# Seven edits to a Mamba layer followed by an attention and convolution layer: loads, state copies, plan constants, last image

## The chip, the cores and the metric

The kernel runs on one core of one Trainium2 chip, in fp32 throughout. The metric is device time in microseconds (us), lower is better: the median over the runs of a kernel. One more execution was recorded by the hardware profiler; durations and stages in this document come from that one.

## The reference, cut to what matters

Four images of 512 channels x 32 x 32 go through two residual layers. Before each layer the image is normalised by groups of 16 channels.

```
x = x + mamba(_gn(x), ...)      # layer 0
x = x + pab(_gn(x), ...)        # layer 1

def mamba(f):                    # tokens: L = 1024, C = 512, d_inner = 1024, 16 states
    xn = layernorm(tokens(f)) * ln_w + ln_b
    xm, z = split(xn @ W_in)
    xs = silu(causal_conv4(xm) + conv_b)
    proj = xs @ W_x                              # 32 dt ranks, 16 B rows, 16 C rows
    dt = softplus(proj[:32] @ W_dt + b_dt);  A = -exp(A_log)
    h[t] = exp(dt[t] * A) * h[t-1] + dt[t] * xs[t] * B[t]     # for each channel and state
    y[t] = sum over states of h[t] * C[t]
    return ((y + xs * D) * silu(z)) @ W_out

def pab(x):
    map = softmax over all pairs of (conv1x1(x, w_center)^T conv1x1(x, w_top))
    x = x + map applied to conv3x3(x, w_bottom)
    return conv3x3(x, w_out)
```

## The kernel before, in words

**Two stages.** Layer 0 for all four images comes first, then layer 1 image by image. The normalised images between the two go through DRAM tiles `x1[b][h]`.

**Layer 0.** An image is 1024 tokens long and is scanned in two halves (h = 0 and 1) of T = 512. The 1024 inner channels are cut in 8 blocks of 128 and taken in pairs (e = 0 to 3). So one image is 8 stretches n = 2e + h, and each stretch is 16 units, one per state s; the four images are 32 stretches of 16 units. In a unit (function `unit`), for each of the two channel blocks j:

- ScalarE makes the decay exp(dt * A) (L746), in SBUF (`da`) or, for six of the 16 states, in PSUM (`u`).
- dt * x * B is made in one of two ways. For ten states (`B_ON_ACT`) ScalarE scales transposed rows (`sc`, L758) and TensorE turns them back into a PSUM tile `u` (L784). For the six others GpSimd multiplies by a broadcast row loaded from DRAM (`dbx`, L773).
- VectorE runs the scan along the tokens (L798). In stretches with h = 0 the last column is saved in `carry_sb` as the start of the half h = 1. For three states (`C_ON_DVE`) the scan's result is in the PSUM tile `u` and each scan is followed by its own one-column copy (L803). For the 13 others the result is in SBUF, and one copy of two columns follows when both scans of the unit are done (L820).
- The product with C is made by VectorE for the three states (L814) and by GpSimd for the others (L826). TensorE then adds the product, transposed, into the PSUM accumulators `y0` and `y1` (L833).

At the end of a stretch, `gate` copies y out (L856), turns it back and multiplies by silu(z). Beside the scans of one image run the group norm and layer norm of the next (`norms`), its input projections and convolutions (`conv1`), its x projections (`params`: 16 matmuls, L652), the projections of z (`gates`), the output projection of the last image (`out_proj`), and a transform of the 3x3 weights of layer 1 (`transform`, 32 pieces, each two ScalarE scalings L1084 and L1085, twelve GpSimd operations, three loads and twelve stores).

**What sets the order.** The order within each engine's queue in layer 0 is written by `Plan.issue`. Every step has a priority in units of the scan (`prio`), an assumed duration and a ring of buffers; the planner walks a simulated clock and, on each engine, takes the step of lowest priority value among those that could start soonest. A transform is a `fill` step. Offsets of priorities lie in `PRM`. GpSimd's, ScalarE's and SyncE's DMA queues run in order too. All rings are small: `u` has four PSUM tiles, `h` and `dbx` four SBUF tiles each, `cbc` (the C rows) six.

**The start.** The first image is loaded in four chunks of channels through SyncE's queue, between loads and stores of the transforms. The small weights are loaded on ScalarE's and GpSimd's queues.

**Layer 1.** For each image: 3x3 convolution `w_bottom` (`conv3`, in a Winograd form: six row positions p in three pairs, four column positions q, 96 weight tiles of 1 MB per convolution kind in all), attention (`attend`), scores of the next image, 3x3 convolution `w_out`, and `finish`, which turns the result back (L1470), adds it to `x1` loaded again from DRAM (L1463, L1475) and stores it (L1480). The order here is the program's order as the framework's own scheduler arranges it.

Of the kernel before, what the change touches and what calls it, by code (L numbers as in the profile page):

```python
# [8 lines left out]
F32 = mybir.dt.float32  # L9
AF = mybir.ActivationFunctionType  # L10
# [5 lines left out]
P = 128  # L16
B, C, HH, WW = 4, 512, 32, 32
L = HH * WW
NCC = C // P
# [11 lines left out]
PRM = dict(fi=4.61, m0=27.7, n0=50.77, nl=1.39, q0=50.1, qg=7.76, c0=53.17, cg=7.07, p0=120.48, e0=6.38, eg=3.72, g0=78.98, gg=9.04, o0=14.48, og=4.13, dl=9.01, t0=10, tg=21.42)  # L31
# [24 lines left out]
class Plan:  # L56
# [5 lines left out]
    HOP, LOAD, SLACK, AHEAD = 0.05, 1.3, 0.05, 17.64  # L62
# [107 lines left out]
def mamba_then_pab_kernel(  # L170
# [33 lines left out]
    nc.sync.dma_start(gm_sb, gmat)  # L204
# [8 lines left out]
    nc.gpsimd.dma_start(wt_sb[:, :, 0, :], w_top.rearrange("(c p) n -> p c n", p=P))  # L213
    nc.gpsimd.dma_start(wt_sb[:, :, 1, :], w_center.rearrange("(c p) n -> p c n", p=P))
    pb_sb = cpool.tile([P, 1], F32, tag="pb", name="pb_sb")
    nc.gpsimd.dma_start(pb_sb[0:PAB], b_top)
    nc.gpsimd.dma_start(pb_sb[PAB:P], b_center)
# [46 lines left out]
    with ExitStack() as l0:  # L264
# [16 lines left out]

        mean_w = wp.tile([P, P], F32, tag="mean_w", name="mean_w")
        nc.vector.memset(mean_w, 1.0 / C)

        def small(src, name, cols):
            t = wp.tile([P, cols], F32, tag=name, name=name)
            nc.scalar.dma_start(t, src)
            return t

        lnw_sb = small(ln_w, "lnw_sb", NCC)  # L290
# [5 lines left out]
        a_sb = small(a_log, "a_sb", NDC * NS)  # L296
# [3 lines left out]
        nc.vector.tensor_scalar_mul(a_sb, a_sb, -1.0)  # L300

        wx_sb = wp.tile([P, NDC, RK + 2 * NS], F32, tag="wx", name="wx_sb")
        nc.scalar.dma_start(wx_sb, w_x.rearrange("(d p) n -> p d n", p=P))
# [4 lines left out]
        for k in range(2):  # L308
            nc.gpsimd.memset(wdt_sb[k], 0.0)
            nc.scalar.dma_start(wdt_sb[k][k * NP : k * NP + RK, :], w_dt)  # L310
# [10 lines left out]
        def dram_set(name, shape, n=B):  # L321
# [8 lines left out]
            "xt": 1, "xs": 10, "win": 2, "yt": 1, "dt": 2, "dtx": 2, "dtxt": 2, "cbc": 6,  # L330
# [30 lines left out]
        carry = [buf(None, None, "") for s in range(NS)]  # L361
# [26 lines left out]
        def norms(b, prio, lag=0.0):  # L388

            t = xts[b] = buf("xt", [P, NCC, L], f"xt_{b}")  # L390
            src = x[b].rearrange("(c p) h w -> p c (h w)", p=P)
            for c in range(NCC):
                step(
                    "SP", 0.3, lambda c=c: nc.sync.dma_start(t()[:, c, :], src[:, c, :]),
                    [], [t], prio, kb=512,
                )
# [27 lines left out]
            def mid():  # L424
# [26 lines left out]
                [stat], [pv], prio, "exp",  # L451
# [121 lines left out]
        def project(b, k, w, name, hs, prio, p=None, at=0, holds=()):  # L573
            t = xts[b]
            return group(
                name,
                [
                    (
                        lambda c=c: w()[:, c, :], lambda c=c: t()[:, c, hs],
                        [w, ready[b][c]],  # L580
                    )
                    for c in range(NCC)
                ],
                prio, hs.stop - hs.start, [t, *holds], p, at,
            )
# [37 lines left out]
        def gates(b, d, prio):  # L623

            w = load_win(b, NDC + d, prio)
            sz = buf("sz", [P, L], f"sz_{b}_{d}")
            for h, hs in enumerate(halves):
                p = project(b, NDC + d, w, f"pz_{b}_{d}_{h}", hs, prio)
                step(
                    "ACT", 0.48,  # L630
                    lambda hs=hs, p=p: nc.scalar.copy(sz()[:, hs], p()),  # L631
                    [p], [sz], prio,
                )
            step(
                "ACT", 0.97, lambda: nc.scalar.activation(sz(), sz(), AF.Silu),
                [], [sz], prio, "silu",
            )
            step(
                "SP", 0.3, lambda: nc.sync.dma_start(szd[b][d // 2][:, d % 2, :], sz()),
                [sz], [szds[b][d]], prio, kb=512,  # L640
            )

        def params(b, prio):
# [3 lines left out]
            for h, hs in enumerate(halves):  # L647
                pp = buf("mm" if b else f"y{h}", [P, T], f"pp_{b}_{h}")
                for d in range(NDC):
                    step(  # L650
                        "PE", MM,
                        lambda d=d, hs=hs, pp=pp: nc.tensor.matmul(  # L652
                            pp()[p0 : p0 + NP, :], wx_sb[:, d, :], xs[b, d]()[:, hs],
                            start=(d == 0), stop=(d == NDC - 1),
                        ),
                        [xs[b, k] for k in range(NDC)] if b and d == 0 else [xs[b, d]], [pp],
                        prio if b else prio - 10 + d + 0.5,
                    )
                step(
                    "ACT", 0.48,  # L660
                    lambda hs=hs, pp=pp: nc.scalar.copy(pr()[:, hs], pp()[p0 : p0 + NP, :]),
                    [pp], [pr], prio,
                )
            step(
# [19 lines left out]
        def delta(b, e, h, prio):  # L684
# [29 lines left out]
            for j in range(2):  # L714
                pt = buf("mm", [P, NK, P], f"pdt_{name}_{j}")

                def turn(j=j, pt=pt):
# [6 lines left out]
                    [pt], [dtxt], prio,  # L724
# [3 lines left out]
        def unit(b, e, h, s, y):  # L728
# [49 lines left out]
            for j, u in enumerate(us):  # L778
                part = parts[j]
                if on_act:  # L780
# [11 lines left out]
                    step("PE", 4 * TR, turn, [sc], [u], prio - 1)  # L792
                else:
                    step("ACT", EXP, lambda j=j, u=u: decay(j, u()), [dt], [u], prio - 1, "exp")

                def scan(j=j, u=u):
# [5 lines left out]
                    if h == 0 and on_dve:  # L802
                        nc.vector.tensor_copy(carry_sb[:, j, s : s + 1], ht[:, T - 1 : T])  # L803

                before, behind = ([carry[s]], []) if h else ([], [carry[s]] if on_dve else [])
                step(
                    "DVE", SCAN + (0.15 if behind else 0.0), scan,
# [9 lines left out]
            if h == 0 and not on_dve:  # L817
                step(
                    "DVE", 0.15,
                    lambda: nc.vector.tensor_copy(carry_sb[:, :, s], hc()[:, :, T - 1]),  # L820
                    parts, [carry[s]], prio - 1, holds=[hc],
                )
# [6 lines left out]
            for j in range(2):  # L829
# [9 lines left out]
                step("PE", 4 * TR, add, [parts[j]], [y[j]], prio, holds=[hc])  # L839
# [87 lines left out]
        xv = [x[b].rearrange("(c p) h w -> p c (h w)", p=P) for b in range(B)]  # L927
# [62 lines left out]
        def first_image(prio):  # L990
# [11 lines left out]
            step("POOL", 1.2, make, [], [pieces, *chunks], prio)  # L1002
            for c in range(NCC):
                for h in range(NH):
# [7 lines left out]
                        [x1s[0][h]], [chunks[c]], prio, kb=512,  # L1012
# [53 lines left out]
        def transform(u, src, k, prio):  # L1066
# [20 lines left out]
            step("ACT", 0.83, scales, [], [ends, mids], prio, fill=True)  # L1087
# [45 lines left out]
        norms(0, -200)  # L1133
# [41 lines left out]
    with ExitStack() as l1:  # L1175
# [15 lines left out]

        brow = []
        for name, src in (("b", b_bottom), ("o", b_out)):
            t = wp.tile([1, C], F32, tag=f"brow_{name}", name=f"brow_{name}")
            nc.scalar.dma_start(
                t.rearrange("o (c p) -> o c p", p=P), src.rearrange("p (c o) -> o c p", o=1)
            )
            nc.scalar.activation(t, t, AF.Copy, scale=2.0 / ALPHA[1])
            brow.append(t)
# [118 lines left out]
        def conv3(name, xg, u, bias, first=None):  # L1318
# [47 lines left out]
            for pair in PAIRS:  # L1366
# [14 lines left out]
                for k, p in enumerate(pair):  # L1381
                    m = {}
                    for q in (2, 1, 0, 3):
                        w = fp.tile([P, NCC, C], F32, tag="u", name=f"uw_{name}_{p}_{q}", bufs=3)
# [21 lines left out]
                    ns.append(n)  # L1406

                if pair == (0, 5):
                    nc.gpsimd.tensor_add(y[0], y[0], ns[0])
                    nc.gpsimd.tensor_add(y[3], y[3], ns[1])  # L1410
                    break
# [44 lines left out]

        def finish(b, y):

            dst = out[b].rearrange("(c p) h w -> p c (h w)", p=P)
            for j in range(NCC):  # L1460
                o = fp.tile([P, L], F32, tag="f4", name=f"o_{b}_{j}")
                for h in range(NH):
                    nc.sync.dma_start(  # L1463
                        o[:, h * T : (h + 1) * T], x1[b][h][j * P : (j + 1) * P, :]
                    )
                ov = o.rearrange("p (i r j k) -> p r k i j", r=4, j=TJ, k=2)
                for rr in range(2):
                    pt = ps.tile([P, 4, P], F32, tag="ps", name=f"po_{b}_{j}_{rr}")
                    for k in range(4):
                        nc.tensor.transpose(  # L1470
                            pt[:, k, :], y[2 * rr + k // 2][:, k % 2, j * P : (j + 1) * P], ident
                        )
                    for k in range(2):
                        o2 = ov[:, 2 * rr + k]
                        nc.vector.tensor_add(  # L1475
                            o2, o2, pt[:, 2 * k : 2 * k + 2].rearrange(
                                "p k (i j) -> p k i j", j=TJ
                            ),
                        )
                nc.scalar.dma_start(dst[:, j, :], o)  # L1480
# [3 lines left out]
        for b in range(B):  # L1484
# [6 lines left out]
            if b + 1 < B:  # L1491
                st, rp = scores(b + 1, image[b + 1])
            finish(b, conv3(f"o{b}", xg, uo, brow[1], v))
# [58 lines left out]
```

## Time and profile before

| what | value |
|---|---|
| median of 3 runs | 3147.45 us (3142.55 to 3149.4) |
| profiled execution: its own time | 3152.2 us |
| profiled execution: its span | 3150.4 us |
| start, until the first `dtx` (the last step before the scans) | 151.94 us |
| 32 stretches of scans, until the copy of the last y | 151.94 to 2095.19 us |
| from there to the first matmul of layer 1's first convolution | 2095.19 to 2136.88 us |
| layer 1, until the last matmul | to about 3134 us |
| PE, DVE, ACT, POOL busy over the span | 89%, 74%, 60%, 69% |
| mean granted TensorE clock | 0.968 |

PE is TensorE, DVE VectorE, ACT ScalarE, POOL GpSimd and SP SyncE. A row of groups gives the line, the engine, the operation, output and inputs, the count, then the busy time, the mean ns of one, and the idle time of that engine just before, with what ended it. A row of the stage table gives the stretch and then, for each engine, busy time and number of instructions, the clock, the share of time the DMA engines moved data and the rate. A row of the timeline gives start, duration, engine, line, operation and, in brackets, the idle time before it.

### The profile page before, as it was taken

The page shows a single profiled execution, that of the slowest core. Times are in us where ns is not written, and L with a number is a line of the kernel's source. Part 1 is how long each engine was busy: PE and PEld are TensorE (multiplying, and loading weights), DVE is VectorE, ACT ScalarE, POOL GpSimd, SP SyncE. Part 2 cuts the span into 40 slices and gives each one's busy share as a digit, 9 for nine tenths or more (in the row PEclk, how much of TensorE's full clock was granted, in tenths as well). Part 3 has the DMA queues.
Part 4 walks back from the last instruction along what each step waited for, and adds up shares of the span by engine and source line. Part 5 has one row for each costly group of instructions (what it writes and reads, how often), then busy time and mean ns, then how long its engine had stood idle before and what let it go on. Part 6 is the DMA issues. An engine that isn't in the chain of part 4 may idle for free. (4 is left out here: it accounts for less than half of the span.)

```text
span 3150.4 us, 36613 instructions
## 1 busy us (share of the span) xinstructions
PE 2801.1 (89%) x11832; PEld 1654.8 (53%) x11832; DVE 2324.9 (74%) x2746; ACT 1896.9 (60%) x3322; POOL 2185.6 (69%) x1207
## 2 busy tenths in 40 slices
PE   4988878989888999888999877779999999999998
PEld 2455656666556656565655655544444444444443
DVE  3488899988999988999987987876275366447344
ACT  3499889998799999789998787752030030020000
POOL 8899898999969999978899998853052142224222
PEclk8999899999999999999999989989999999999999
DMA  6666455577645567745567654457268448628817
GB/s 190 192 186 195 144 152 162 156 226 241 212 118 169 163 204 250 231 114 155 165 192 227 204 172 123 121 139 263 93 225 312 183 147 317 257 74 312 321 61 253
DMA packets 401414, 600.03 MB, mean 190 GB/s; under 512 B 47176, under 2 KB 241992, under 8 KB 376648
## 3 DMA queue, kind: packets, MB, share of 16 engines
q1 hardware_dynamic: 392128, 582.13, 58.8%
q10 hardware_dynamic: 8936, 15.31, 1.3%
q8 instruction: 94, 1.54, 0.2%
q14 instruction: 96, 0.79, 0.1%
q0 software_dynamic: 160, 0.26, 0.0%
HBM read 500.60 MB, written 96.99 MB: 190 GB/s over the span
## 5 line engine op out<-in xcount | busy, mean ns | idle before, releaser
L826 POOL TENSOR_TENSOR da<-da,cbc 128x1024 f32<-128x1024 f32 x288 | 679.4, 2364 | 87.2 <-DVE carry_sb L820 47.4
L758 ACT ACTIVATE sc<-dtxt,bt_sb 128x256 f32<-128x256 f32 x1280 | 557.1, 496 | 49.3 <-PE u L784 48.8
L746 ACT ACTIVATE da<-dt,a_sb 128x512 f32<-128x512 f32 x640 | 439.4, 713 | 70.1 <-PE y L833 69.5
L773 POOL TENSOR_TENSOR dbx<-dtx,bbc 128x1024 f32<-128x1024 f32 x192 | 452.1, 2367 | 30.6 <-DMA bbc<-bcd 8.3
L784 PE MATMUL u<-ident,sc 128*128 128x128 f32 x2560 | 380.6, 282 | 52.4 <-DVE da L798 31.7
L833 PE MATMUL y<-ident,da 128*128 128x128 f32 x2560 | 357.3, 283 | 70.7 <-POOL da L826 68.2
L798 DVE TENSOR_TENSOR_SCAN da<-da,carry_sb,u 128x512 f32<-128x512 f32 x288 | 353.3, 1260 | 82.8 <-PE u L784 82.6
L833 PEld LDWEIGHTS y<-ident,da 128*128 128x128 f32 x2560 | 297.6, 145 | 183.4 <-POOL da L826 134.2
L784 PEld LDWEIGHTS u<-ident,sc 128*128 128x128 f32 x2560 | 302.2, 144 | 160.3 <-issue 41.7
L798 DVE TENSOR_TENSOR_SCAN da<-da,u 128x512 f32<-128x512 f32 x288 | 337.1, 1202 | 37.3 <-PE u L784 37.2
L1389 PE MATMUL m_b<-uw_b,v_b 128*128 128x512 f32 x768 | 339.1, 599 | 10.3 <-DMA uw_b<-u_b 9.4
L1389 PE MATMUL m_o<-uw_o,v_o 128*128 128x512 f32 x768 | 333.5, 595 | 4.3 <-DVE v_o L1311 4.1
L826 POOL TENSOR_TENSOR dbx<-dbx,cbc 128x1024 f32<-128x1024 f32 x128 | 302.8, 2365 | 32.1 <-DVE carry_sb L820 22.6
L381 PE MATMUL pxm<-xt,winc 128*128 128x344 f32 (+2 forms) x768 | 249.6, 469 | 30.5 <-DVE xs L610 13.9
L746 ACT ACTIVATE u<-dt,a_sb 128x512 f32<-128x512 f32 x384 | 252.9, 679 | 34.8 <-DVE da L798 18.9
L833 PE MATMUL y<-ident,dbx 128*128 128x128 f32 x1536 | 217.1, 281 | 43.7 <-POOL dbx L826 31.6
L381 PE MATMUL pz<-xt,winc 128*128 128x512 f32 x512 | 246.2, 599 | 10.5 <-ACT sz L631 3.1
L1389 PEld LDWEIGHTS m_b<-uw_b,v_b 128*128 128x128 f32 x768 | 144.7, 191 | 197.8 <-issue 185.7
L1389 PEld LDWEIGHTS m_o<-uw_o,v_o 128*128 128x128 f32 x768 | 145.5, 190 | 190.5 <-issue 181.2
L833 PEld LDWEIGHTS y<-ident,dbx 128*128 128x128 f32 x1536 | 178.4, 144 | 98.2 <-POOL dbx L826 48.6
L1437 PE MATMUL pat<-y_b,st 128*128 128x512 f32 x512 | 221.7, 593 | 0.1
L1397 ACT ACTIVATE e_b<-m_b 128x512 f32<-128x512 f32 x24 | 14.3, 596 | 320.6 <-PE m_b L1389 299.4
(231 smaller groups left out, 4536.2 us busy)
## 6 DMA issues: line engine op xcount, KB each, us to landing
cbc<-bcd SPq DMA_DIRECT2D x512, 256.0 KB, 3.7
uw_b<-u_b SPq DMA_DIRECT2D x96, 1024.0 KB, 4.9
uw_o<-u_o SPq DMA_DIRECT2D x96, 1024.0 KB, 4.9
bbc<-bcd SPq DMA_DIRECT2D x192, 256.0 KB, 4.1
u_b<-work SPq DMA_DIRECT2D x192, 128.0 KB, 2.3
u_o<-work SPq DMA_DIRECT2D x192, 128.0 KB, 3.1
winc<-in_w_in_dram SPq DMA_DIRECT2D x64, 256.0 KB, 3.8
szd<-sz SPq DMA_DIRECT2D x32, 512.0 KB, 3.6
```

Source lines behind the costliest of these rows:

```text
L381: lambda k=k, lhs=lhs, rhs=rhs: nc.tensor.matmul(p()[:, at : at + cols], lhs(), rhs(), start=(k == 0), stop=(k == n - 1)),
L746: nc.scalar.activation(t, dt()[:, j], AF.Exp, scale=a_sb[:, at : at + 1])
L758: nc.scalar.activation(sc()[:, k], dtxt()[:, k], AF.Copy, scale=bt()[:, at, s : s + 1])
L773: lambda: nc.gpsimd.tensor_mul(hc(), dtx(), b_bc().to_broadcast([P, 2, T])),
L784: nc.tensor.transpose(u()[:, k * P : (k + 1) * P], sc()[:, k, j, :], ident)
L798: nc.vector.tensor_tensor_scan(ht, *((hc()[:, j], u()) if on_act else (u(), hc()[:, j])), carry_sb[:, j, s : s + 1] if h else 0.0, ALU.mul ...
L826: lambda: nc.gpsimd.tensor_mul(hc(), hc(), c_bc().to_broadcast([P, 2, T])),
L833: nc.tensor.matmul(y[j]()[:, k, :], hc()[:, j, k * P : (k + 1) * P], ident, start=(s == 0 and k == 0), stop=(s == NS - 1 and k == NK - 1), ...
L1389: nc.tensor.matmul(m[q], v[:, q, k, c, :], w[:, c, :], start=(c == 0), stop=(c == NCC - 1 and not extra),)
L1397: nc.scalar.activation(e, m[2], AF.Copy, scale=al / 2)
L1437: nc.tensor.matmul(pt, st[m][:, 2 * P * j + h : 2 * P * (j + 1) : 2], xb[m // 2][:, m % 2, :], start=(m == 0), stop=(m == NMC - 1),)
```

## The change

Lines of the changed kernel are shifted by some ten to forty; the text keeps the numbers of the kernel before.

1. **Start.** The four chunks of the first image are the first DMAs on SyncE's queue, before `gmat`. The twelve loads of small weights and of the two score weights move from ScalarE's and GpSimd's queues to SyncE's, behind them. The first norm's steps get spaced priorities (lag 0.01).
2. **Weight scalings behind the first norm.** The ScalarE scalings of all transforms now depend on the first norm's exp (a marker `rooted`), and the projections of z of the first image on the first turned dt x (a marker `begun`).
3. **State copy per scan.** Every scan with h = 0 is followed by its own one-column copy; the two-column copy is gone.
4. **x projections spread.** The 16 matmuls of `params` for images 1 to 3 get priorities 0.29 units apart (`pg`), and start 7.45 units earlier (`p0`).
5. **Turns two units ahead.** The turns into `u` get priority two units ahead of their unit (`kt`) where it was one; the adds into y get 0.64 units more (`ka`).
6. **Other constants.** z projections of the first image earlier and closer (`e0`, `eg`), small shifts of norm, convolution and first image, `cbc` ring of 5.
7. **Layer 1.** The two bias rows are loaded and scaled at the very start (on ScalarE's queue) instead of between the layers. The additions of the last pair into y are cut in halves. The last image loads its `x1` ahead of its last convolution, into buffers of the score tiles; half of its turning back is placed before the last weight's matmuls, the last addition is on VectorE, and the stores alternate between two queues.

```
-PRM = dict(fi=4.61, m0=27.7, n0=50.77, nl=1.39, q0=50.1, qg=7.76, c0=53.17, cg=7.07, p0=120.48, e0=6.38, eg=3.72, ...)
+PRM = dict(pg=0.29, kt=2, ke=1, ka=-0.64, fl=0, fi=-1.28, m0=27.07, n0=50.77, nl=1.81, q0=50.1, qg=7.76, c0=53.17, cg=7.03, p0=113.03, e0=-4.84, eg=3.01, ...)
...
+        first = xtp.tile([P, NCC, L], F32, tag="xt", name="xt_0")
+        for c in range(NCC):
+            nc.sync.dma_start(first[:, c, :], xv[0][:, c, :])
+        nc.sync.dma_start(gm_sb, gmat)
...
-            nc.scalar.dma_start(t, src)
+            nc.sync.dma_start(t, src)
...
-                [stat], [pv], prio, "exp",
+                [stat], [pv] if b else [pv, rooted], prio, "exp",
...
-            step("ACT", 0.83, scales, [], [ends, mids], prio, fill=True)
+            step("ACT", 0.83, scales, [rooted], [ends, mids], prio, fill=True)
...
-                        prio if b else prio - 10 + d + 0.5,
+                        prio + PRM["pg"] * (d + NDC * h) if b else prio - 10 + d + 0.5,
...
-                    step("PE", 4 * TR, turn, [sc], [u], prio - 1)
+                    step("PE", 4 * TR, turn, [sc], [u], prio - PRM["kt"])
...
-                    if h == 0 and on_dve:
+                    if h == 0:
                         nc.vector.tensor_copy(carry_sb[:, j, s : s + 1], ht[:, T - 1 : T])
...
-            if h == 0 and not on_dve:
-                step(
-                    "DVE", 0.15,
-                    lambda: nc.vector.tensor_copy(carry_sb[:, :, s], hc()[:, :, T - 1]),
-                    parts, [carry[s]], prio - 1, holds=[hc],
-                )
...
-                step("PE", 4 * TR, add, [parts[j]], [y[j]], prio, holds=[hc])
+                step("PE", 4 * TR, add, [parts[j]], [y[j]], prio - PRM["ka"], holds=[hc])
...
+                    if pair == (0, 5):
+                        eng = nc.vector if late and k else nc.gpsimd
+                        for c in range(2):
+                            eng.tensor_add(y[3 * k][:, c], y[3 * k][:, c], n[:, c])
...
+        def last(b, xg, v):
+            o = [load_sum(b, j, xp, "st") for j in range(NCC)]
+            def late(y):
+                for j in range(NCC):
+                    turn_back(b, j, o[j], y, 0)
+            y = conv3(f"o{b}", xg, uo, brow[1], v, late)
+            for j in range(NCC):
+                turn_back(b, j, o[j], y, 1)
+                (nc.scalar, nc.sync)[j % 2].dma_start(dst[b][:, j, :], o[j])
```

As the two programs are built, ScalarE's queue has 185 table loads where it had 177. VectorE's has 512 one-column copies where it had 96 of these and 208 of two columns. GpSimd does nine transforms before the first `dtx` where it did ten, and as many as before from the second stretch's `dtx` on. The other counts of computing instructions are the same.

## The prediction, written before the changed kernel was run

> **What bounds the kernel now.** I read the profile in this order: the busy times of the page, the stage table cut at the 32 copies of y (L856), the groups, then the timeline at the three seams (start, between the layers, end). No engine bounds the whole. Layer 1 (2137 to 3134 us) is TensorE at 97%, and the change hardly touches it. In the scans the four engines are nearly level, and the leader changes:
>
> ```profile
> span 3150.4 us, 36613 instructions
> ...
> 152.00:223.26 71.26, 58.71 (x301) 38.71 (x302) 51.93 (x61) 65.59 (x116) 67.64 (x38) 0.93 0.69 189
> ...
> 415.45:477.71 62.26, 48.45 (x287) 34.67 (x286) 60.83 (x80) 53.55 (x93) 58.52 (x29) 1.00 0.57 165
> ...
> 716.19:770.57 54.38, 51.22 (x287) 34.03 (x286) 50.01 (x48) 47.34 (x92) 53.75 (x32) 1.00 0.79 237
> ...
> 899.48:970.87 71.39, 61.98 (x317) 43.80 (x318) 64.08 (x90) 63.04 (x106) 47.13 (x22) 0.95 0.45 132
> ```
>
> Columns: stretch, length, then PE, weight loads, DVE, ACT, POOL. POOL leads n = 0 (67.6 of 71.3) and n = 9 (99%), DVE n = 4 (98%); n = 12 is led by nobody. Over all 32 stretches (1943 us) POOL is busy 1760, DVE 1723, ACT 1690. So an engine's saving counts only in the stretches that it leads.
>
> ```profile
> L826 POOL TENSOR_TENSOR da<-da,cbc 128x1024 f32<-128x1024 f32 x288 | 679.4, 2364 | 87.2 <-DVE carry_sb L820 47.4 <-DVE da L798 20.2 <-PE u L784 4.5
> L798 DVE TENSOR_TENSOR_SCAN da<-da,carry_sb,u 128x512 f32<-128x512 f32 x288 | 353.3, 1260 | 82.8 <-PE u L784 82.6
> L820 DVE COPY carry_sb<-da 128x2 f32<-128x2 f32 x144 | 83.8, 582 | 3.9
> L820 DVE COPY carry_sb<-dbx 128x2 f32<-128x2 f32 x64 | 43.3, 676 | 1.6
> L803 DVE COPY carry_sb<-u 128x1 f32<-128x1 f32 x96 | 15.2, 158 | 3.3
> ```
>
> The two-column copies take 127 us of DVE for almost no data; the one-column ones 0.158 us each.
>
> **The change, part by part** (against the profiled execution, 3152.2 us).
>
> *Start.*
>
> ```profile
> 14.34 0.49 SPq L394 DMA_DIRECT2D xt<-in_x_dram  x1
> 20.35 0.21 DVE L411 BATCH_NORM_AGGREGATE mv_l<-bs_l 128x2 f32<-128x12 f32 x1
> 28.29 0.18 ACT L448 ACTIVATE pv_l<-gdev_l 128x4 f32<-128x4 f32 x1
> 151.94 2.50 POOL L710 TENSOR_TENSOR dtx<-dt,xs 128x512 f32<-128x512 f32 x2 [10.41 <-ACT dt L702]
> 166.22 2.33 DVE L798 TENSOR_TENSOR_SCAN da<-da,u 128x512 f32<-128x512 f32 x2 [20.83 <-PE u L784]
> ```
>
> The last chunk of x is issued at 14.3 because it stands behind stores that wait for POOL. In front, the four chunks are issued by 2.5 (0.4 us each in this timeline); 2 MB at the 320 GB/s that the page's best slices show is 6.5 us, so it lands near 9, statistics end near 10.5 instead of 20.6, and the exp of the first norm (28.5) comes about 14 earlier: 10 from the load, 4 because no scaling and no late weight stands in ACT's queue. Down to the layer norm's end (66.3) the halves no longer interleave: pmu's second half, 4.8 of its 9.6 us, runs under VectorE, and two scalings leave ACT; with the first step's wait I put 7. Sum 21: dt is ready at 130.5. The moved loads: 16 more issues on SP of 0.4 us, 7 us, put the first transform's loads at 13 or so; POOL starts its first transform near 15, as now (13.96). Nine transforms of 12.4 us (spacing in the timeline) end at 130 with two short waits, so `dtx` starts at about 130.5. But one transform fewer is behind us, and POOL leads n = 0: 12.4 of the 21 are paid back there. Left 9. The marker on the z projections lets the first scan follow `dtx` by about 7 us instead of 14.3, but POOL is full either way, so I add only 1: **-10**. Bounds: -5 (eight gates now crowd ACT in n = 0, which is at 92%) and -21.
>
> *State copies.* A rule of the Trainium skill speaks against this part. The row first:
>
> ```profile
> 764.92 4.68 POOL L826 TENSOR_TENSOR da<-da,cbc 128x1024 f32<-128x1024 f32 x2
> 767.43 2.19 DVE L820 COPY carry_sb<-da 128x2 f32<-128x2 f32 x1
> ```
>
> The copy lasts until POOL's operation ends (769.60 and 769.62): it waits for it. "SBUF — State Buffer" (Who interferes with whom) says why: a VectorE copy in the two-port mode and a GpSimd operation exclude each other for a whole instruction. "VectorE: DVE Perf Modes" (What auto-detection actually checks) says when: source and destination in SBUF, with outermost sizes even or equal. L803's 0.158 us are of copies out of PSUM, which the rule exempts; the new ones copy from SBUF, and one column equals one column. By the rule the 416 new copies wait as the 208 do, at 0.61 us mean: 254 us, 127 more than now. By the nearest row in size, L803, they take 416 x 0.158 = 66 us, 61 less. No row shows a one-column copy out of SBUF beside POOL. I take 0.158: a single element has no second half for a second port; both ends stay in the range's reasons. At 61 less, an h = 0 stretch saves its copies' time (2.3 to 10.8 us in the stage table of L820) less 26 x 0.158 = 4.1. In those that DVE leads (n = 2, 4, 6, 12, 20, 30) that sums to 13; in those where POOL or ACT is within 4 us of it (8, 10, 14, 16, 18, 22) to 25, of which I count a third. **-20**, bounds -61 and +85 (two thirds of 127: the h = 0 stretches leave DVE only 98 us of idle time).
>
> *Turns.* DVE waits 119.8 us for turns (L784), 99 without the first. One unit earlier on PE they should meet their scans, but they sit longer in the four `u` tiles, and the adds put off by 0.64 units hold `da` longer, for which ACT already waits 69.5 us. I take a tenth of the 99: **-10**, bounds -50 and +30.
>
> *x projections* (16 x 2 matmuls of 0.43 us in a block of 7 us of PE, three times) spread between turns: **-3**. *Eight more table loads*: the row is 1.28 us with the next ACTIVATE 0.02 after its end (149.51, 1.28; 150.81), 10.3 us of ACT; "ScalarE: Activation LUTs" (What ACT_TABLE_LOAD costs) has 2.66 with the drain, 21. I take the row; ACT leads a third of the stretches: **+3** (by the page +7).
>
> *Between the layers.*
>
> ```profile
> 2099.20 1.24 ACTq L1195 DMA_DIRECT2D brow_b<-in_b_bottom_dram  x1
> 2105.18 0.63 ACT L1198 ACTIVATE brow_b<-brow_b 1x512 f32<-1x512 f32 x1 [8.55 <-DMA brow_b<-in_b_bottom_dram]
> 2107.44 5.71 PE L381 MATMUL po<-xs,wpr 128*128 128x512 f32 x8 [4.60 <-ACT grstd_image L245]
> ```
>
> Without the bias row in ACT's queue the norm's root is 6 us earlier, but VectorE now adds all four output blocks before normalising: twelve more matmul records of 7.4 us from 2102.8, an add, four normalisations of 0.75, 16 matmuls of 6.9 from 2111.8 end at 2118.7, not 2121.75. **-3**.
>
> *End.*
>
> ```profile
> 3134.61 2.36 POOL L1410 TENSOR_TENSOR y_o<-y_o,n_o 128x1024 f32<-128x1024 f32 x1 [11.32 <-DVE n_o L1405]
> 3145.41 1.41 DVE L1475 TENSOR_TENSOR o<-o,po 128x256 f32<-128x256 f32 x4 [5.17 <-DMA o<-x]
> ```
>
> After: 16 early turns of 0.11 put the last convolution result at 3136.3, two adds of 0.67 on DVE, 0.5 of turns, eight adds of 0.41 end at 3141.5 where they end at 3146.8 now. **-5**. The early `x1` loads wait on SyncE for the last score tiles, ahead of weight tile 4 of the last convolution; its buffer is free only at 3054, when these eight issues (3.2 us from 3044) are over: nothing. The halved additions of the other images: nothing, PE has the next image's matmuls there.
>
> Sum: -10 - 20 - 10 - 3 + 3 - 3 - 5 = -48, or 3104 for the profiled execution; the median stands 4.75 below it: **3099**.
>
> **The rivals.** (a) *Only the seams pay* (0.25): POOL, at 91% in the scans, does no less work, so DVE's saving becomes DVE idle time. -10 - 3 - 5, and a few from turns: 3125, range 3112 to 3141. For: POOL's 1760 us and the level loads. Against: POOL itself waits 70 us for L820. (b) *More comes free* (0.18): with short copies POOL's waits for L820 (47.4 + 22.6) and DVE's for turns both shrink by half, and the start keeps 15: 3060, range 3040 to 3079. (c) *Slower: the one-column copies queue behind POOL* (0.08, by the rule above): +85 - 31 gives 3201. It decides at a mean copy of 0.42 us: then 416 x 0.42 - 127 = 48 more on DVE, two thirds of which eats the other 31. (d) *No change* (0.03): a change that does not do what it says; the built order shows the copies, the loads and the turns moved, so only a balance of (a) and some lateness gives it. The likeliest (0.46): 3080 to 3112.
>
> **How the numbers follow.** The measurement can tell 0.2%, 6.3 us, from no change. Faster: 0.46 + 0.18 + 0.25 = 0.89, and a little of (c) when its copies are cheap, 0.90. Same 0.03. Slower 0.07. The range leaves out most of (c) and the far half of (b), and takes in (a) nearly whole: 3061 to 3135.
>
> **What would show it.** In the profile after: last `xt` issue before 3 us; first `dtx` near 130 and the copy of the first y near 213; one-column copies at 0.16 us mean, with none that ends with a POOL operation (above 0.42 the forecast falls to (c)); DVE's wait for L784 below 100; POOL's wait for copies gone but partly turned into waits for scans; last add near 5 us before the place it has now against the last matmul. If the stretches with h = 0 are not shorter by 1 to 3 us each, (a) holds.

## The result, and the profile after

| | before | changed |
|---|---|---|
| median | 3148.43 us (4 runs, 3142.55 to 3156.02) | 3105.28 us (4 runs, 3101.93 to 3106.01) |
| ratio to before | | 0.986, 95% interval 0.9837 to 0.9882 |
| profiled execution: span | 3150.4 us | 3103.9 us |

The change makes the kernel 43 us faster; 3099 was predicted, within 3061 to 3135. The two profiled spans differ by 46.5 us. They are cut here at the same marks as in the prediction:

| part | before | changed | difference | predicted |
|---|---|---|---|---|
| until the first y is copied | 223.26 | 229.17 | +5.9 | -10 |
| stretches n = 1 to 31 | 1871.93 | 1834.78 | -37.2 | -30 (copies -20, turns -10, x projections -3, tables +3) |
| to the first matmul of layer 1's convolution | 41.7 | 39.4 | -2.3 | -3 |
| from there to the last matmuls of the last attention | 906.4 | 898.0 | -8.4 | 0 |
| from there to the end | 107.1 | 102.6 | -4.5 | -5 |

So the sum was right, the two small seams were right, and the first term had the wrong sign. The stage table of the changed kernel, for the stretches that the prediction showed (n = 0, 4, 9 and 12; columns as before: stretch, length, PE, weight loads, VectorE, ScalarE, GpSimd):

```profile
144.10:229.17 85.07, 78.60 (x347) 47.84 (x348) 47.88 (x72) 78.53 (x129) 80.27 (x52) 0.96 0.76 221
...
406.98:467.61 60.63, 51.35 (x290) 38.07 (x289) 57.89 (x91) 54.25 (x93) 58.99 (x30) 0.94 0.55 165
...
699.34:751.31 51.97, 49.68 (x278) 33.68 (x277) 44.69 (x46) 46.32 (x87) 51.50 (x31) 1.00 0.78 251
...
869.56:942.77 73.21, 66.64 (x350) 46.99 (x349) 71.16 (x114) 69.37 (x115) 52.13 (x24) 0.99 0.48 132
```

n = 4, which VectorE led with 98%, is 1.6 us shorter and GpSimd leads it now; n = 9, led by GpSimd, is 2.4 shorter; n = 12 is longer. The largest single gains are elsewhere: n = 2 (77.89 to 64.69), n = 19 (66.83 to 56.40), n = 11 (67.34 to 59.36). Two of them are handed on: n = 20 gives 8.7 back, and n = 11 to 13 together take 199 us in both kernels. Of the 37.2 us, 22.8 are gained in n = 1 to 8.

*The copies.* The groups of the changed kernel:

```profile
L829 DVE COPY carry_sb<-da 128x1 f32<-128x1 f32 x288 | 44.2, 154 | 9.9
L829 DVE COPY carry_sb<-dbx 128x1 f32<-128x1 f32 x128 | 19.7, 154 | 4.4
L829 DVE COPY carry_sb<-u 128x1 f32<-128x1 f32 x96 | 15.2, 158 | 3.3
```

The 416 new copies out of SBUF last 154 ns, at most 157, as long as those out of PSUM: 79 us in all where the copies took 142. The timeline shows two of them beside a busy GpSimd:

```profile
745.88 7.00 POOL L846 TENSOR_TENSOR da<-da,cbc 128x1024 f32<-128x1024 f32 x3
...
746.62 1.20 DVE L824 TENSOR_TENSOR_SCAN da<-da,u 128x512 f32<-128x512 f32 x1
747.85 0.15 DVE L829 COPY carry_sb<-da 128x1 f32<-128x1 f32 x1
...
749.18 0.15 DVE L829 COPY carry_sb<-da 128x1 f32<-128x1 f32 x1
```

GpSimd is busy from 745.88 to 752.88; both copies run and end inside. The rival in which they queue behind GpSimd is out. The rule that spoke for it ("VectorE: DVE Perf Modes" of the Trainium skill, What auto-detection actually checks) puts its condition on outermost sizes other than one, and the prediction left "other than one" out; a copy of one column has no such size beside its partitions, and here the measurement decides: no one-column copy waited.

*The start.* SyncE's queue, ScalarE, VectorE and GpSimd in the timeline of the changed kernel:

```profile
0.72 1.98 SPq L291 DMA_DIRECT2D xt<-in_x_dram  x4
...
3.42 0.47 SPq L299 DMA_DIRECT2D a_sb<-in_a_log_dram  x1
12.26 0.33 SPq L299 DMA_DIRECT2D lnw_sb<-in_ln_w_dram  x1
...
19.47 1.04 SPq L1098 DMA_DIRECT2D work<-in_w_bottom_dram  x2
```

```profile
11.10 0.21 DVE L433 BATCH_NORM_AGGREGATE mv_l<-bs_l 128x2 f32<-128x12 f32 x1
12.27 0.63 ACT L221 ACTIVATE brow_b<-brow_b 1x512 f32<-1x512 f32 x1 [6.26 <-DMA brow_b<-in_b_bottom_dram]
18.33 0.18 ACT L470 ACTIVATE pv_l<-gdev_l 128x4 f32<-128x4 f32 x1
26.05 1.82 POOL L1111 TENSOR_TENSOR work<-work 128x768 f32<-128x768 f32 x1 [21.86 <-ACT work L1103]
138.19 1.06 ACT L728 ACTIVATE dt<-dt 128x1024 f32<-128x1024 f32 x1
144.10 2.49 POOL L736 TENSOR_TENSOR dtx<-dt,xs 128x512 f32<-128x512 f32 x2
157.11 1.22 DVE L824 TENSOR_TENSOR_SCAN da<-da,u 128x512 f32<-128x512 f32 x1 [22.54 <-PE u L810]
```

The statistics end at 11.3 (10.5 predicted). But SyncE issues nothing between 3.9 and 12.26, the moment at which the first bias row has landed. The list of SyncE's waits in this stretch names the cause:

```profile
SPq L299 <- DMA brow_b<-in_b_bottom_dram: 8.4, 1, 8.4
```

The load of `lnw_sb` has no use for the bias row. It is the ninth load of the program, the bias row is the first, and in the trace both count their landing on the same semaphore (the counter by which a program waits): the ninth load is held until the first has landed. The kernel before has the same kind of wait, and its profile showed it; here a load of `winc` waits for `cb_sb`, which came through ScalarE's queue:

```profile
SPq L568 <- DMA cb_sb<-in_conv_b_dram: 1.4, 1, 1.4
```

So in the changed kernel the loads of the first transform are issued at 19.5 (13 was assumed) and GpSimd starts it at 26.05 (15 was assumed). ScalarE's queue is held by the same row: the exp of the first norm ends at 18.51, where 14.5 was predicted. Nine transforms of 12.4 us follow with 6.7 us of gaps, and `dtx`, whose dt is ready at 139.25, waits for GpSimd until 144.10.

### The profile page after: what moved, and what is told of

Its sections match the earlier page's. It is cut to its first block, busy times and chain, and to the rows that moved or that the text cites. A ratio compares the mean times of both kernels' runs of the same rounds, so it can differ in the third digit from the quotient of the medians.

```text
span 3103.9 us, 36778 instructions
## 1 busy us (share of the span) xinstructions
PE 2788.6 (90%) x11832; PEld 1654.8 (53%) x11832; DVE 2273.7 (73%) x2956; ACT 1902.3 (61%) x3331; POOL 2179.9 (70%) x1217
## 5 line engine op out<-in xcount | busy, mean ns | idle before, releaser
L824 DVE TENSOR_TENSOR_SCAN da<-da,u 128x512 f32<-128x512 f32 x288 | 349.2, 1213 | 52.8 <-PE u L810 45.4
L772 ACT ACTIVATE u<-dt,a_sb 128x512 f32<-128x512 f32 x384 | 254.1, 679 | 12.3 <-DVE dbx L824 6.0
L1410 ACT ACTIVATE e_b<-m_b 128x512 f32<-128x512 f32 x24 | 14.3, 596 | 311.9 <-PE m_b L1402 290.6
```

Of the source, the lines that this page charges most:

```text
L772: nc.scalar.activation(t, dt()[:, j], AF.Exp, scale=a_sb[:, at : at + 1])
L824: nc.vector.tensor_tensor_scan(ht, *((hc()[:, j], u()) if on_act else (u(), hc()[:, j])), carry_sb[:, j, s : s + 1] if h else 0.0, ALU.mul ...
```

## The experiments

Each comparison is with the kernel before, run on the same chip; the changed kernel stands at 0.986. A difference between a variant and the changed kernel is one of medians, and is given by ratios or spans too where these say something else. Differences below 0.2% between two variants are not taken for real unless the trace shows the cause.

**State copy per scan alone, on the kernel before.** Two-column copy out, `if h == 0:` and one state marker for each channel block in.

> The kernel before with the state copy per scan alone (512 one-column copies in place of 96 of one column and 208 of two). Theory A (the two-column copies waited for GpSimd, and VectorE's time counts where it leads): VectorE's copies fall from 142 to about 79 us, none of them over 0.2 us, and the kernel gains 15 to 25 us, about 3128. Theory B (GpSimd's work sets the pace of the scans, so VectorE's saved time turns into idle time): the copies are as short, but the gain is below 6 us, 3143 to 3149.

Measured: 3143.28 against 3146.35, ratio 0.9993 (0.9986 to 0.9999). All 512 copies last 153 to 159 ns, yet almost nothing is gained: theory B by its number. But not by its reason. Many stretches with h = 0 are 2 to 4 us shorter (n = 4, 6, 8, 10, 16, 18, 24), and up to the end of n = 8 this kernel is 11.6 us ahead of the kernel before. Then two stretches with h = 1 are longer by 10.9 and 6.5 (n = 9 and 17), and late ones with h = 0 by 4.0 and 7.0 (n = 26 and 30). The stage row of n = 9, then VectorE's waits in it:

```profile
704.56:769.85 65.29, 58.40 (x294) 38.25 (x295) 47.26 (x49) 49.23 (x93) 60.87 (x35) 0.97 0.78 243
```

```profile
DVE res L910 <- PE po L381: 15.9, 4, 5.7
```

A whole block of the output projection has moved from n = 8 into n = 9: 66 records of `po` in n = 9, 29.8 us of TensorE (the kernel before has 47 and 22.9 us there, the changed kernel 48 and 22.3), and none in n = 8 (18 and 17). VectorE, in its fixed order, stands 15.9 us behind four additions to `res` that wait for it. The kernel before has 2.3 us of that in its n = 9, the changed kernel 1.2.

**Two-column copy back, in the changed kernel.**

> The changed kernel with the two-column copy put back; all else stays. Theory A: slower than the changed kernel by 15 to 25 us, about 3125, with copies of up to 2.7 us that end with a GpSimd operation. Theory B: within 6 us of it, 3102 to 3111.

Measured: 3132.06, ratio 0.9954 (0.9941 to 0.9967): 27 us slower than the changed kernel (22.5 by the two spans), as theory A says. Its timeline:

```profile
759.96 4.68 POOL L799 TENSOR_TENSOR dbx<-dtx,bbc 128x1024 f32<-128x1024 f32 x2
...
763.21 1.46 DVE L846 COPY carry_sb<-da 128x2 f32<-128x2 f32 x1
```

The copy ends (764.67) with GpSimd's pair (764.64). The 208 copies take 128.1 us, as before. So the copy is worth 27 us beside the other edits and 3 on the kernel before: something else in the change makes its gain collectable. (Another copy step also changes the written order, so the 27 us are those of waiting and of order together.)

**Turns one unit ahead again, adds not put off.** `kt=2, ka=-0.64` to `kt=1, ka=0`.

> The changed kernel with the turns one unit ahead of their unit again and the adds into y not put off (kt = 1, ka = 0). If the early turns are worth what the prediction gave them: 10 us slower, about 3115, and VectorE's wait for turns rises from some 116 us toward 120 to 140. If they are worth nothing without the freed VectorE, or cost as much by holding tiles as they give: 3103 to 3108. If they carry most of the gain of the scans: 3120 or more.

Measured: 3104.99, ratio 0.9874 (0.9857 to 0.9891). The turns alone are worth nothing that can be told (without them the kernel is 0.3 us faster by the medians, 4 slower by the ratios); VectorE waits for them 115.7 us (101.4 + 14.3) where the changed kernel waits 116.0 (95.8 + 20.2) and the kernel before 121.0 (119.8 + 1.2).

**Bias rows loaded as columns.** The rows leave ScalarE's queue; the columns go behind the small weights and are turned into rows by eight small TensorE matmuls between the layers:

```
-        nc.scalar.dma_start(t.rearrange("o (c p) -> o c p", p=P), src.rearrange("p (c o) -> o c p", o=1))
-        nc.scalar.activation(t, t, AF.Copy, scale=-12.0)
+            nc.sync.dma_start(bcol[:, k, :], src)
...
+                nc.tensor.matmul(pr[:, c * P : (c + 1) * P], bcol[:, k, c : c + 1], ident, start=(c == 0), stop=(c == NCC - 1))
+            nc.vector.tensor_scalar_mul(brow[k], pr, -12.0)
```

> The changed kernel, with the two bias rows of layer 1 loaded as columns (128 pieces of 16 bytes each, on SyncE's queue behind the small weights) and turned into rows by TensorE between the layers, where the changed kernel loads them as rows at the start (512 pieces of 4 bytes each, on ScalarE's queue). Theory A (these 1024 small pieces hold up SyncE's issues from 3.9 to 12.3 us): SyncE issues on without the gap, the first transform starts on GpSimd at about 18 to 19 us in place of 26, the first y is 5 to 8 us earlier, and the total 3098 to 3101. Theory B (SyncE's queue is held up by its own loads of x): the gap stays, the total is within 3 us of 3105.

Measured: 3099.06, ratio 0.9847 (0.9833 to 0.9862). SyncE's queue, ScalarE and GpSimd in its timeline:

```profile
3.62 0.44 SPq L293 DMA_DIRECT2D lnw_sb<-in_ln_w_dram  x1
...
5.65 0.43 SPq L293 DMA_DIRECT2D cb_sb<-in_conv_b_dram  x1
8.09 0.33 SPq L293 DMA_DIRECT2D bdt_sb<-in_b_dt_dram  x1
9.41 0.33 SPq L293 DMA_DIRECT2D dp_sb<-in_d_param_dram  x1
...
14.66 0.18 ACT L466 ACTIVATE pv_l<-gdev_l 128x4 f32<-128x4 f32 x1
21.91 1.80 POOL L1107 TENSOR_TENSOR work<-work 128x768 f32<-128x768 f32 x1 [17.72 <-ACT work L1099]
```

The gap of 8.4 us is gone; 3 us in two pieces remain, and these are waits for the loads of x, so theory B holds for a part:

```profile
SPq L293 <- DMA xt<-in_x_dram: 3.0, 2, 2.0
```

Here too each of the two loads that wait (`bdt_sb`, `dp_sb`) stands eight places behind the chunk of x that it waits for. The exp of the first norm ends at 14.84 (the prediction's number), the first transform starts 4.1 us earlier (less than the 7 to 8 expected), the first y comes at 225.30, 3.9 earlier. The two rows were 1024 pieces of four bytes. "DMA: Bandwidth & Descriptors" of the Trainium skill (Rules for kernel authors) says that a load with a strided last dimension becomes one descriptor, that is one piece, per element. A row landed 11.5 us after its issue here, a column load 1.9. The variant changes piece size, queue and place in the order at once, so what each of them is worth is not shown; what the wait was for is.

**x projections in one block again.** `pg=0.29, p0=113.03` to `pg=0, p0=120.48`.

> The changed kernel with the x projections of images 1 to 3 in one block again (pg = 0, p0 = 120.48). The state copies alone gained 0.1% on the kernel before, and taking them back from the changed kernel lost 27 us, so they need a partner. Theory C (the partner is the spread of the x projections: a block of 7 us of TensorE makes late what freed VectorE could have taken): 15 to 25 us slower than the changed kernel, about 3125, the loss in the stretches where the projections stand. Theory D (the partner is the fit of the written order as a whole, or the small constants): 3103 to 3111, no more than the 3 us that the prediction gave.

Measured: 3107.12, ratio 0.9877 (0.9863 to 0.9891). Theory C is out: the copies do not need the spread as their partner. The difference is 2 us by the medians, 5 by the ratios and none by the spans.

**Four small constants back.** `AHEAD` 17.64 (how far the planner looks ahead), `m0=27.7`, `nl=1.39`, `cg=7.07`.

> The changed kernel with four small constants of the order as they were before (planner's window 17.64, m0 = 27.7, nl = 1.39, cg = 7.07). Theory C: within 5 us of the changed kernel. Theory D (constants were fitted to the copy per scan): 10 to 25 us slower, with single stretches 5 to 12 us longer where a step stands in a queue ahead of its input, as in the kernel before with the copies alone (stretch n = 9, 65.3 us in place of 54.4, VectorE waiting 15.9 us for output projections).

Measured: 3099.83, ratio 0.985 (0.9837 to 0.9864): not slower, if anything faster, so these four constants are no partner that is needed either. They move work between neighbours: n = 12 and 20 become 69.3 and 68.1 (73.2 and 80.3 in the changed kernel), n = 11 and 19 become 67.0 and 67.5 (59.4 and 56.4).

**The old start in the changed kernel.** Loads, queues and order as before; no markers; `e0=6.38, eg=3.72`.

> The changed kernel with the start of the kernel before: chunks of x, small weights and scalings in their old order and queues, no markers, z projections of the first image at their old priorities, bias rows loaded between the layers again. By the prediction's start of -10 and seam of -3 it would be 13 us slower, 3118. By the two traces, which show the first y 5.9 us later after the change, it would be 3 us faster (6 gained at the start, 2.3 lost between the layers, all within the noise of a reordered first image): 3097 to 3106.

Measured: 3110.9, ratio 0.9893 (0.9878 to 0.9908), span 3107.6. The expectation from the two traces was wrong. The first y is indeed earlier, at 222.63, but then:

```profile
284.20:356.23 72.03, 55.47 (x271) 38.05 (x270) 64.40 (x108) 64.06 (x107) 59.24 (x34) 0.86 0.54 164
356.23:417.51 61.28, 52.21 (x298) 41.87 (x297) 55.42 (x65) 57.12 (x103) 56.54 (x33) 0.89 0.51 148
```

n = 2 and 3 take 133.3 us, in the changed kernel 117.5. At the end of n = 3 the changed kernel is 10.5 us ahead (406.98 against 417.51). So the new start pays, later than where it was looked for. Why these two stretches are shorter was not tested. One thing moves with it: ScalarE loads tables twice in n = 2 of the changed kernel and 14 times in n = 0; with the old start it is 8 and 7 times, in the kernel before 7 and 7, at 1.28 us each. (In this variant the loads of the bias rows are issued at the start too, at 6.3 and 9.4 us; the last chunk of x goes out at 16.0, 1.6 us later than in the kernel before.)

**Halved additions alone, on the kernel before.**

> The kernel before with the additions of the last pair into y cut in halves, for all images, on GpSimd; nothing else. The prediction gave them nothing. If TensorE's waits for GpSimd's addition (3.8 us of matmul and 6.3 us of weight loads in layer 1 of the kernel before, three each) are what shortened layer 1 by 8.4 us after the change: 4 to 8 us faster, 3138 to 3142. If the prediction was right: 3144 to 3148.

Measured: 3143.63 against 3146.85, ratio 0.999 (0.9982 to 0.9999): 3 us, below the 4 to 8 expected. TensorE's weight loads wait for that addition, before (without the last image) and then with halves (with it):

```profile
PEld po L1470 <- POOL y_o L1410: 6.3, 3, 2.1
```

```profile
PEld po L1471 <- POOL y_o L1409: 3.9, 4, 1.2
```

Three waits of 2.1 us become three of 0.9, and the last image's, at the very end, goes from 1.5 to 1.2: some 4 us. The rest of the 8.4 cannot be put down to the change. With the copies alone, where layer 1 is untouched, the same part took 899.6 us in its profile where the kernel before took 906.4, with 6.7 us of waiting for weights instead of 9.4; and with the changed layer 1 it took up to 904.8 (the last variant below).

**Copy alone, with the output projection's additions later.** On the first of these variants, `res` and its store get `at + 1.5`.

> The kernel before with the copy per scan, as in the run that gained 0.1%, and with one thing more: VectorE's additions of the output projection (res) and their stores get a priority 1.5 units later. Theory E (in that run the freed VectorE stood at these additions, which wait in its queue for TensorE: 40.8 us in place of 24.2): the wait falls to 25 or less, stretches n = 9 and n = 17 come back to about 54, and the kernel gains 12 to 18 us on the kernel before, 3129 to 3135. Theory F (the loss is TensorE's and GpSimd's work that has moved across the stretch's end): the wait falls, the time stays within 5 us of 3143.

Measured: 3148.39 against 3147.99, ratio 0.9996 (0.9985 to 1.0007). It tested little: in the written order the additions of n = 9 kept their places (only some of the later images moved, by a few scans), VectorE still waits 42.1 us for output projections, and n = 9 takes 66.1. Theory E is neither shown nor refuted by it.

**Turns, x projections and small constants all back, in the changed kernel.** What stays is the start, the copies, layer 1 and the ring of five C rows.

> The changed kernel with turns, x projections and the four small constants all back together; what stays of the change is start, copy per scan, layer 1 and the ring of five C rows. Each alone moved the changed kernel by -5 to +2 us. If the copies need any one of them as a partner: 3115 to 3130. If the copies gain by themselves as soon as the order does not stand in their way, and the run on the kernel before met one bad order: 3097 to 3107.

Measured: 3122.41, ratio 0.9914 (0.9898 to 0.993): 17 us slower than the changed kernel, though each alone cost nothing that could be told. The stage row of its n = 9, then VectorE's waits in it:

```profile
693.28:759.96 66.68, 60.51 (x297) 38.94 (x298) 48.61 (x51) 49.24 (x93) 62.20 (x36) 0.97 0.77 240
```

```profile
DVE res L936 <- PE po L401: 15.9, 4, 5.7
```

This is the pattern of the copies alone, to the microsecond: 15.9 us of waiting in n = 9, and n = 17 takes 61.2 us (61.0 there). All 24 additions to `res` stand at the same places between the scans in both runs. With any two of the three edits in place the pattern is gone, as the three runs above show; with none of them, 17 of the copies' 27 us are lost. What one of them alone would do was not tried. `fi`, the ring of five C rows and the start were never taken back together with them.

**Bias columns and the old small constants together.**

> The two gains found so far together: bias rows loaded as columns (3099) and the four small constants as before (3100). If they are independent, as start and later images should be: 3092 to 3096.

Measured: 3098.64, ratio 0.9836 (0.9817 to 0.9855). The first y comes at 221.25, but the total is that of the columns alone: the two do not add, and that the four constants gained anything by themselves is not shown.

**The last variant, with the loads of layer 1 behind unit 40 as well.**

> The same, and the six loads that only layer 1 reads (two score weights, two score biases, two bias columns) are issued on SyncE behind unit 40 of the first image instead of ahead of the first transform. They take 3.5 us of SyncE's issues at 11.4 to 14.7 us; if GpSimd's first transform sets the start, it begins at 18 to 19 us instead of 22, and the total is 2 to 4 us lower again, 3088 to 3093. If the first norm's exp (14.7 us) or something behind it sets it: no change.

Measured: 3092.72 (3090.46 to 3094.79), ratio 0.9818 (0.98 to 0.9837), span 3090.6: the fastest of all, each of its four runs below each of the changed kernel's. GpSimd in its timeline:

```profile
18.72 1.81 POOL L1101 TENSOR_TENSOR work<-work 128x768 f32<-128x768 f32 x1 [14.53 <-ACT work L1093]
```

Against the variant before, which has columns and constants too, it is 6 us faster (2 to 4 were expected): the first transform starts 2.5 us earlier and the first y comes at 217.35, 3.9 earlier. Against the changed kernel these are 7.3 and 11.8 us. dt is ready at 129.30, and `dtx` follows the last transform at 134.19 without a gap on GpSimd: GpSimd, and with it the time of its first transform, sets the start.

## Why the prediction was right in its sum

The sum fits in part by luck. The start was 16 us worse than predicted, the stretches 7 and the first part of layer 1 8 us better, and of these last 8 the change explains about half.

*Start: -10, and its working failed.* The failing step is "POOL starts its first transform near 15, as now". It started at 26.05, and `dtx` came at 144.10 where 130.5 was predicted: 13.6 of the 16 us. The estimate counted the issue time of the moved loads (7 us; there are fourteen of them), not the 8.4 us in which SyncE was held for a bias row that it did not need; the variant without the rows gave half of that back at the first transform. GpSimd had the same work until the first y (191.9 us busy before, 189.7 after), so a start 12 us later on GpSimd ate what the load of x had brought. dt was late too, at 139.25 for 130.5, behind an exp of the first norm that came 4 us late; in the last variant, where this exp ends at 14.64, dt is ready at 129.30, as predicted. The other 2.4 us lie in n = 0. That the marker "lets the first scan follow `dtx` by about 7 us" was wrong: it followed by 13.0. 115 records of z projections fell into n = 0 where 61 had been, TensorE and ScalarE were busy 78.6 and 78.5 of its 85.1 us, and the stretch took 13.8 us longer, where 12.4 less 1 was predicted. One reading of the profile was off as well: the stores ahead of the last chunk of x did not wait for GpSimd but for a load of the transform's weights:

```profile
SPq L1119 <- DMA work<-in_w_bottom_dram: 4.3, 1, 4.3
```

What the prediction did not look for is that n = 2 and 3 became shorter. Through n = 3 the changed kernel is 8.5 us ahead of the kernel before, and the old start put back costs 4 us by the spans, 6 by the medians and 10 by the ratios. That this comes near 10 is luck.

*Copies: -20.* The duration was right to 4 ns (158 taken, 154 measured), and the choice of the nearest row against the rule was right. What it is worth is not one number: 27 us beside the other edits, 3 alone. That 20 lies between the two is luck: the step that counted "a third" of the stretches led by others knew nothing of the order.

*Turns: -10.* Measured: nothing that can be told by themselves, and VectorE's wait for them did not fall below 100 us, which was to be the sign; it is 116. *x projections: -3.* 0 to -5, within the noise. The step that failed for both is to price each edit by itself: taken back one by one they cost nothing, and 17 us as a group with the constants, because the others keep the order out of the bad place. The rival "only the seams pay" is out: stretches 1 to 31 are 37 us shorter after the change, and still 17 us shorter, by the trace, with the two-column copies put back.

*Tables: +3.* The eight loads are there, at 1.28 us each. The count puts nine more ahead of the first y and one fewer behind it, so they belong to the start and n = 0 and not to the later stretches. Their price was not measured by itself.

*Between the layers -3, end -5.* Measured -2.3 and -4.5, by the steps that were given: the last eight additions end at 3098.2, 4.8 us behind the start of the last group of turns, with no wait for a load among them.

*Halved additions: nothing.* About -3 to -4. The step "PE has the next image's matmuls there" is wrong; the wait of the turns for GpSimd's addition stood in the trace of before, three times 2.1 us.

Two small slips in the sums do not move the forecast: the saving in the second group of stretches adds up to 23 and not 25 us, and in rival (c) the other terms are -28 and not -31, as the tables were left out.

What stays open: why the order of the kernel before, with short copies, puts a block of the output projection one stretch later. The experiment that was to move VectorE's additions did not, so it is not shown by itself that the moved block costs the time, and which of the three edits keeps it away by which step was not traced.

## What to carry to other kernels

Where four engines are level and their order is written out, price a group of edits together: the same copies gave 3 us or 27, and three edits that cost nothing when taken back singly cost 17 together. At a start, look first at the queue that feeds the first busy engine, and at the list of what it waits for: here a slow load on another queue held it, though nothing on it used that load. In this kernel a copy of 128x1 next to a busy GpSimd never waited, and one of 128x2 did: it pays to copy one column at a time.

## What the hardware showed that was not expected

Two loads of 512 pieces of four bytes on ScalarE's queue were issued at 0.7 and 2.0 us, and the first had landed only at 12.3; between the layers of the kernel before, the same load took 6.0 us. As 128 pieces of 16 bytes each on SyncE's queue, loads of the same values landed after 1.9 us. SyncE's idle 8.4 us are no matter of its queue: the program waited there for the bias row. Copies of two columns took from 0.155 to 2.78 us, the long ones beside GpSimd; copies of one column never took more than 0.16.
